# Four stacked graph layers on one core: the first tiles of the last projection between the last sums of layer 3, and the mask sums of a layer's first block between the first pair's tiles

## The chip, the cores and the metric

The kernel runs on one core of a Trainium2 chip. The core has five engines that run their own queues in order and meet through semaphores: TensorE (PE, matmul; its weight loads are shown as PEld), VectorE (DVE), ScalarE (ACT), GpSimd (POOL) and SyncE (SP, which here only issues transfers). The metric is the device time of one execution in microseconds (us), the median of several runs. Less is better.

## The reference

The input is a matrix x of 2708 rows and 512 columns and a symmetric 0/1 adjacency of 2708 x 2708 with a full diagonal. Four layers follow each other, each as x = layernorm(x + f(x, adj)). Layers 0 and 1 are sums over neighbours with linear maps. The change concerns layers 2 and 3, which are graph attention.

```python
# layer 2, and the first half of layer 3: 8 heads of 64 columns each
Wh = einsum('nf,hfo->hno', x, W)
e = leaky_relu(src[:, :, None] + dst[:, None, :], 0.2)   # src, dst: Wh times a vector, per head
attn = softmax(where(adj > 0, e, -9e15), axis=-1)
h = einsum('hnm,hmo->hno', attn, Wh)
...
# layer 3 goes on
x1 = elu(h), heads side by side                           # [2708, 512]
h2 = the same attention with one head of 512 columns, weights Wo, ao
out = relu(elu(h2) @ lin1 + b1) @ lin2 + b2
x = layernorm(x + out)
```

## The kernel before, in words

Rows are cut into NT = 22 tiles of P = 128 rows (the last has 20). The transposed mask lies in SBUF as fp8 (maskT). All phases are written one after another in one Python function. A scheduler of the framework then orders each engine's queue, so an instruction may stand earlier in its queue than its place in the text. Two things hold it: data and buffers, and chains by hand. The function pe() chains matmuls in program order, each after the one before it. A second means, tc.issue_after, places what is issued in it after a named instruction.

The order of phases for layers 2 and 3 is: project("p2"), heads_attention("a2"), project("p3"), heads_attention("a3"), project("p4"), last_attention. The last one holds the one-head attention and the two linear maps.

**project** takes the 22 input tiles one at a time. For each it has a transposed input xT, multiplies it with the weights (L561, 16 matmuls), and makes from the result the columns dcol, ucol, ecol, vcol and the values R2 that the attention uses. The helper early() makes inputs ahead of need. For p4 the input is made by elu_turned, two tiles at a time.

**heads_attention** works on two blocks of output columns: tiles 0 to 10 (1408 columns) and 11 to 21 (1300 columns). Within a block it goes by pairs of heads, four pairs a block, so eight runs. A run loops over the 22 row tiles j. For each j and each of the two heads:

- DVE makes the unnormalised weights e (L624), from a broadcast row v_bc, a column of ucol, and the mask. There are five e buffers.
- ACT makes c from e (L632, a sigmoid with a huge scale, so 0 or 1): which of the two branches of the leaky_relu holds.
- PE adds R2 times e into po (L782), 12 matmuls for the two heads.
- After every four j, PE adds c times parts_c into pd (L697, "divisors").

The softmax's divisor of each column is put together from these divisor sums and from a sum over the mask alone. The mask sums are the products of masks() (L680, 88 matmuls for a block), a copy, a small matmul (fold) and a copy into rcs (keep, L689). For the second block they stand already between the tiles of a pair, at j = 12, 16 and 20. For the first block they stand ahead of the first pair:

```python
            products, fold, keep = masks(0, pd[1])
            for step in (*products, fold, keep):
                step()
            todo = {}
```

After a pair, finish() lays its steps over the tiles of the next pair (the dictionary todo, by j): the last divisors (rest), fold, divide (which ends with a reciprocal into rcs). In layer 3 the summed features are sent to the DRAM tensor oT_dram as they stand, transposed and undivided. At the last pair of a block, spread transposes the reciprocals, copies them to a tile r and sends them, head by head, to rc_dram (L752).

**elu_turned** reads both back. It loads o from oT_dram (L833) and the reciprocals rc from rc_dram, broadcast over partitions (L835, two loads), multiplies (L837, DVE), takes exp (L838, ACT), and finishes the elu with two DVE steps (L839, L840). Its o buffers, four of two tiles each, are the last 4096 of the 10240 columns of the tile lin, which lies in memory that the attention of layer 3 has used. The first part of lin takes the weights of the first linear map, 2 MB, loaded by the GpSimd queue (L858).

The last line of project checks that all values lie in a range and counts them into okc. The sum of the counts must equal expected.

Of the kernel before, what the change touches and what calls it, by code (L numbers as in the profile page):

```python
# [2 lines left out]

# [15 lines left out]
P = 128  # L19
D = 512  # L20
# [10 lines left out]
def kernel(  # L31
# [59 lines left out]


    o_dram = dram.tile([N, D], F32, name="o_dram")
    oT_dram = dram.tile([D, N], F32, name="oT_dram")
    rc_dram = dram.tile([H, NT * P], F32, name="rc_dram")

    behind = []

# [54 lines left out]
    def early(first, n, make):  # L153

        made = {}

        def get(i, **how):
            for j in range(len(made), min(i + first + 1, n)):
                made[j] = make(j, **how)
            return made[i]  # L160
        return get
# [337 lines left out]
    rcs = late.tile([P, 2, H, 12], F32, name="rcs")  # L499
    okc = const.tile([P, 4], F32, name="okc")  # L500
    nc.vector.tensor_scalar(rdeg, iso, 0.0, None, op0=OP.is_equal, op1=OP.add, accum_out=okc[:, 3:4])
    expected = float(P * NT * (3 * H + 1))

    def split(pool, dst, src):

# [7 lines left out]
    def project(name, source, layer, v_dram, cuts, turned=None):  # L513
# [12 lines left out]
        with ExitStack() as ph:  # L526
# [5 lines left out]
            xs = early(1, NT, lambda t: source(sm, t, rows(t)))  # L532
            xTs = early(0, NT, lambda t: transposed(ahead, ps_tr, xs(t), rows(t), "xT"))
            if turned:
                twos = early(2, -(-NT // 2), lambda i: turned(sm, 2 * i, min(2 * i + 2, NT)))
                xTs = lambda t: twos(t // 2)[:, :, t % 2 * P:t % 2 * P + P]
            vrows, bs = {}, {}

            def keep_v(t):
# [52 lines left out]
                                                    -1.0, None, op0=OP.mult)  # L592
                            split(sm, pairs_c[:, a:z, :, k, 6 * k + 3:6 * k + 6], ecol[:, a:z, k::2])
            keep_v(NT - 1)
            sq = sm.tile([P, NT, H], F32, name="sq", bufs=1)
            if heads < H:
                nc.vector.memset(sq, 0.0)
            dd = dcol[:, :, :heads]
            nc.vector.tensor_mul(sq[:, :, :heads], dd, dd)
            sq = sq.rearrange("p t h -> p (t h)")  # L600
            nc.vector.tensor_scalar(sq, sq, RANGE * RANGE, None, op0=OP.is_le, op1=OP.add,
                                    accum_out=okc[:, layer:layer + 1])

# [31 lines left out]
    nb = 2  # L635
    cuts = [-((-NT * i) // nb) for i in range(nb + 1)]
    blocks = list(zip(cuts[:-1], cuts[1:]))

    def heads_attention(name, att, as_rows):

        with ExitStack() as ph:
# [56 lines left out]
            def finish(b, h0, p, pair, oT):  # L700

                t0, t1 = att.blocks[b]
                nt = t1 - t0
                feats, cols = slice(h0 * HO, (h0 + 2) * HO), slice(t0 * P, t0 * P + att.width(b))
                got = {}

                def rest():
                    divisors(b, p, pair)
                    got["dT"] = copied(p)

                def fold():
                    got["sums"] = folded(got["dT"], pick_c.rearrange("p g k q -> p (g k q)")).rearrange(
                        "p t g (k q) -> p t g k q", k=2)

                def divide():
                    sums, r = got["sums"], rcs[:, b, h0:h0 + 2, :]
                    rc = sm.tile([P, 2, 12], F32, name="rc")
                    by = rc.rearrange("p k (g t) -> p t g k", g=4)
                    nc.vector.tensor_mul(by, sums[:, :, :, :, 1],
                                         vcol[:, t0:t0 + 12, h0:h0 + 2].rearrange("p (g t) k -> p t g k", g=4))  # L720
                    nc.vector.tensor_add(by, by, sums[:, :, :, :, 0])
                    nc.vector.tensor_add(rc, rc, r)
                    nc.vector.tensor_scalar(rc, rc, 1e-30, None, op0=OP.max)
                    nc.vector.reciprocal(r, rc)

                def turn(a0):
                    ps = got[a0] = ps_t.tile([P, 512], F32, name="ps_t").rearrange("p (t c) -> p t c", c=P)
                    for t in range(a0, min(a0 + 4, nt)):
                        n = rows(t0 + t)
                        pe(nc.tensor.transpose(ps[:n, t - a0, :], oT[:, a0 // 4, (t - a0) * P:(t - a0) * P + n], ident))  # L730

                def store(a0):
                    a1, full, ps = min(a0 + 4, nt), min(t1, FULL) - t0, got[a0]
                    o = ahead.tile([P, KD, P], F32, name="xT")
                    for n, a, z in [(P, a0, min(a1, full)), (rows(NT - 1), max(a0, full), a1)]:
                        if a >= z:
                            continue
                        nc.scalar.copy(o[:n, a - a0:z - a0], ps[:n, a - a0:z - a0])
                        r0 = (t0 + a) * P
                        rows_ = o_dram[r0:r0 + (z - a - 1) * P + n, feats]  # L740
                        if n == P:
                            nc.sync.dma_start(rows_.rearrange("(t p) c -> p t c", p=P), o[:, a - a0:z - a0])
                        else:
                            nc.sync.dma_start(rows_, o[:n, a - a0])

                def spread():
                    ps = ps_t.tile([P, 512], F32, name="ps_t")
                    pe(nc.tensor.transpose(ps[:12 * H, :P], rcs[:, b].rearrange("p h t -> p (h t)"), ident))
                    r = sm.tile([12 * H, P], F32, name="r", bufs=1)
                    nc.scalar.copy(r, ps[:12 * H, :P])  # L750
                    for h in range(H):
                        nc.gpsimd.dma_start(rc_dram[h, t0 * P:t1 * P].rearrange("(t p) -> t p", p=P),  # L752
                                          r[12 * h:12 * h + nt])

                steps = {0: [rest], 4: [fold], 6: [divide]}
                if as_rows:
                    for a0 in range(0, nt, 4):
                        steps[8 + a0] = [lambda a0=a0: turn(a0)]
                        steps[9 + a0] = [lambda a0=a0: store(a0)]
                else:  # L760
                    nc.gpsimd.dma_start(oT_dram[feats, cols], oT.rearrange("p i c -> p (i c)")[:, :att.width(b)])
                    if h0 == H - 2:
                        steps[8] = [spread]
                return steps

            products, fold, keep = masks(0, pd[1])
            for step in (*products, fold, keep):
                step()
            todo = {}
            for r, (b, h0) in enumerate(runs):  # L770
                w = att.width(b)
                parts = [(c, min(c + 4 * P, w)) for c in range(0, w, 4 * P)]
# [1 line left out]
                vs = [att.load(b, h) for h in hs]  # L774
                po = [ps_o.tile([P, 512], F32, name="po", tag="po") for _ in parts]
                pair = []
                for j in range(NT):
                    es = [att.weights(b, h, j, v) for h, v in zip(hs, vs)]
                    cs = [att.above(b, h, j, e) for h, e in zip(hs, es)]
                    for i, (c0, c1) in enumerate(parts):  # L780
                        for k, (h, e) in enumerate(zip(hs, es)):
                            pe(nc.tensor.matmul(po[i][HO * k:HO * k + HO, :c1 - c0], R2[:, j, h * HO:(h + 1) * HO],  # L782
                                                e[:, c0:c1], start=(j == 0), stop=(j == NT - 1)))
                    if len(pair) == 4:
                        divisors(b, pd[r % 2], pair)
                        pair = []
                    pair.append((j, hs, cs))
                    for step in todo.get(j, ()):
                        step()
# [26 lines left out]
    def summed(sm, t, n):  # L816
# [7 lines left out]
        nc.gpsimd.dma_start(x3_dram[t * P:t * P + n, :], o)  # L824
        return o

    def elu_turned(sm, t0, t1):

        w = sum(rows(t) for t in range(t0, t1))
        cols = slice(t0 * P, t0 * P + w)  # L830
        o = lin[:, -KD * 1024:].rearrange("p (i k n) -> p i k n", i=4, k=KD)[:, t0 // 2 % 4]
        rc = sm.tile([P, KD, 2 * P], F32, name="rc2")
        nc.sync.dma_start(o[:, :, :w], oT_dram.rearrange("(k p) n -> p k n", p=P)[:, :, cols])  # L833
        for q in range(2):
            nc.sync.dma_start(rc[HO * q:HO * q + HO, :, :w],  # L835
                                rc_dram.rearrange("(k q) n -> q k n", q=2)[q, :, cols].partition_broadcast(HO))
        nc.vector.tensor_mul(o[:, :, :w], o[:, :, :w], rc[:, :, :w])  # L837
        nc.scalar.activation(rc[:, :, :w], o[:, :, :w], AF.Exp)  # L838
        nc.vector.tensor_scalar(rc[:, :, :w], rc[:, :, :w], 1.0, -1.0, op0=OP.min, op1=OP.add)  # L839
        nc.vector.scalar_tensor_tensor(o[:, :, :w], o[:, :, :w], 0.0, rc[:, :, :w], op0=OP.max, op1=OP.add)  # L840
        return o
# [116 lines left out]
    for i, source in enumerate((plain, summed)):  # L958
        with ExitStack() as ph:
            att = Weights(ph, f"a{2 + i}", blocks, vd[i])  # L960
            project(f"p{2 + i}", source, i, vd[i], blocks)
            heads_attention(f"a{2 + i}", att, i == 0)
    ph4 = fast.enter_context(ExitStack())
    att = Weights(ph4, "a4", quads, vd[2])
    lin = ph4.enter_context(tc.tile_pool(name="lin", bufs=1)).tile([P, KD * FF + KF * D + KD * 512], F32, name="lin")
# [329 lines left out]
```

## Time and profile before

| | before |
|---|---|
| median of 3 runs | 3096.92 us (3095.4 to 3097.85) |
| profiled run, span | 3089.8 us |
| PE busy | 2969.2 us, 96% |
| DVE busy | 1963.5 us, 64% |
| ACT busy | 1411.1 us, 46% |
| layers 0 and 1 and p2, first instruction to first po | 0 to about 1024 us |
| attention of layer 2, from the first po | 1024.57 to about 1587 us |
| attention of layer 3, from the first po to the last divisors | 1701.49 to 2252.62 us |
| p4, first product | 2279.76 us |

How to read it: a busy share is an average over stages with different limits. In the two attentions of eight heads PE and DVE are both almost full, and which of them sets the pace has to be read from the waits. A line such as "L561" is line 561 of the kernel; "x16" is a number of instructions; a bracket at a line's end tells how long the engine stood before it and what ended the wait. Instruction durations of one engine may overlap a little, so the spacing of two is often less than a duration.

### The profile page before, as it was taken

To read this page: it belongs to the slowest core of one execution; us is meant where nothing else is said; L and a number is where in the kernel's file an instruction comes from. 1 tells how busy PE (TensorE), PEld (TensorE's weight loads), DVE (VectorE), ACT (ScalarE), POOL (GpSimd) and SP (SyncE) were. 2 spreads that over 40 slices of the span, in tenths; PEclk is the share of its full clock that TensorE was granted. 3 is DMA by queue.
4 is the path that set the end of the run, shared out by engine and by line. 5 is a ranking of instruction groups with operands and counts; after the bars stand their busy time and mean duration, and the time that the engine had idled before them with its cause. 6 is when DMAs were issued, how large, how long until landed. Compare 5 with 4: busy or idle time off the path is not lost. (4 is left out here: it accounts for less than half of the span.)

```text
span 3089.8 us, 36801 instructions
## 1 busy us (share of the span) xinstructions
PE 2969.2 (96%) x14714; PEld 1644.4 (53%) x14714; DVE 1963.5 (64%) x2495; ACT 1411.1 (46%) x1590; POOL 239.6 (8%) x378
## 2 busy tenths in 40 slices
PE   8999999999999999999998999999969999999997
PEld 4556666448888433444466333443446455555555
DVE  5662765212233899999976999999944535344242
ACT  2431000112225699999965899999942000001001
POOL 2220010101110000000012000000000000100001
PEclk9999999999999999999999999999989999999999
DMA  6651521312222001011034000000052000000000
GB/s 142 142 124 35 121 67 38 109 60 90 73 74 84 15 29 47 28 38 34 22 107 153 29 29 28 28 27 27 18 156 63 4 14 17 31 14 15 14 21 20
DMA packets 112920, 168.93 MB, mean 55 GB/s; under 512 B 39716, under 2 KB 63141, under 8 KB 112738
## 3 DMA queue, kind: packets, MB, share of 16 engines
q1 hardware_dynamic: 84066, 105.02, 11.4%
q0 software_dynamic: 18784, 57.79, 6.5%
q10 hardware_dynamic: 9888, 3.67, 0.5%
q8 instruction: 118, 1.93, 0.2%
q14 instruction: 64, 0.52, 0.1%
HBM read 136.46 MB, written 44.64 MB: 59 GB/s over the span
## 5 line engine op out<-in xcount | busy, mean ns | idle before, releaser
L624 DVE SCALAR_TENSOR_TENSOR e<-v_bc,ucol,maskT 128x1300 f32<-128x1300 f32 (+3 forms) x836 | 1183.2, 1474 | 335.0 <-PE pn L926 318.8
L632 ACT ACTIVATE c<-e,bcol 128x1300 fp8e4<-128x1300 f32 (+1 forms) x704 | 994.6, 1424 | 82.7 <-DVE e L624 32.8
L782 PE MATMUL po<-e,R 128*64 128x512 f32 (+2 forms) x4224 | 924.9, 549 | 29.9 <-DVE e L624 28.2
L782 PEld LDWEIGHTS po<-e,R 128*64 128x64 f32 x4224 | 349.0, 136 | 573.2 <-issue 383.2
L926 PE MATMUL pn<-e,R 128*128 128x512 f32 (+1 forms) x1056 | 415.1, 544 | 0.0
L926 PEld LDWEIGHTS pn<-e,R 128*128 128x128 f32 x1056 | 192.1, 191 | 199.8 <-issue 196.7
L416 PE MATMUL acc<-yH,kT 128*128 128x512 f32 x484 | 214.8, 444 | 0.0
L894 ACT ACTIVATE w<-pl,b 128x256 f32<-128x256 f32 (+1 forms) x88 | 40.9, 465 | 373.3 <-PE pl L892 373.3
L458 PE MATMUL acc<-yL,mf 128*128 128x512 f32 x484 | 192.9, 399 | 0.0
L416 PE MATMUL acc<-yL,kT 128*128 128x512 f32 x484 | 192.3, 397 | 0.0
L458 PE MATMUL acc<-yH,mf 128*128 128x512 f32 x484 | 190.5, 394 | 0.0
L117 POOL TENSOR_TENSOR ln_rs<-ln_rs,half 128x1 f32<-128x1 f32 x88 | 54.5, 620 | 1676.4 <-DVE ln_rs L116 1674.5
L561 PE MATMUL pm<-w,xT 128*128 128x264 f32 (+1 forms) x704 | 168.3, 394 | 10.7 <-DVE R L575 5.2
L229 PE MATMUL pm<-w,xT 128*128 128x512 f32 (+1 forms) x384 | 173.2, 593 | 2.4 <-ACT xT L130 1.4
L229 PE MATMUL pm<-weight,xT 128*128 128x512 f32 (+1 forms) x352 | 162.0, 604 | 3.6 <-DVE weight L141 2.8
L321 DVE SCALAR_TENSOR_TENSOR kT<-pm,maskT 128x512 fp32r<-128x512 f32 (+1 forms) x132 | 84.8, 642 | 123.5 <-PE pm L319 123.0
L892 PE MATMUL pl<-lin 128*128 128x256 f32 (+1 forms) x704 | 154.8, 374 | 2.8 <-DVE lin L811 2.8
L901 PE MATMUL pl<-lin,w 128*128 128x512 f32 (+1 forms) x352 | 157.4, 593 | 0.0
L561 PEld LDWEIGHTS pm<-w,xT 128*128 128x128 f32 (+1 forms) x704 | 129.6, 189 | 38.0 <-issue 5.8
L892 PEld LDWEIGHTS pl<-lin 128*128 128x128 f32 x704 | 130.6, 192 | 33.4 <-issue 15.8
L455 ACT CAST mf<-maskT 128x1024 fp32r<-128x1024 fp8e4 (+1 forms) x66 | 64.4, 977 | 163.4 <-PE acc L458 154.1
L223 ACT CAST yH<-pm 128x512 fp32r<-128x512 f32 (+1 forms) x44 | 25.7, 585 | 243.6 <-PE pm L229 243.6
(186 smaller groups left out, 2619.9 us busy)
## 6 DMA issues: line engine op xcount, KB each, us to landing
rows<-x_dram SPq DMA_DIRECT2D x63, 256.0 KB
m<-in_adj_dram POOLq DMA_DIRECT2D x21, 677.0 KB, 6.2
v_bc<-v_dram SPq DMA_DIRECT2D x16, 704.0 KB
x_dram<-u POOLq DMA_DIRECT2D x42, 256.0 KB, 2.3
v_bc<-v_dram SPq DMA_DIRECT2D x16, 650.0 KB
rows<-in_x_dram SPq DMA_DIRECT2D x21, 256.0 KB
r_dram<-u POOLq DMA_DIRECT2D x21, 256.0 KB, 3.2
rows<-r_dram SPq DMA_DIRECT2D x21, 256.0 KB
```

Of the source, the lines that this page charges most:

```text
L229: order(nc.tensor.matmul(pm[:n], xT[:, k, :n], w[:, k, :], start=(k == 0), stop=(k == KD - 1)))
L321: nc.vector.scalar_tensor_tensor(kT[:, :w], cum[:, :w], KEEP, maskT[:, j, cols], op0=OP.is_le, op1=OP.mult)
L416: nc.tensor.matmul(pa[t], kT[:, (t - b[0]) * P:(t - b[0] + 1) * P], y[:, j, :], start=(j == 0 and y is yH), stop=(j == NT - 1 and y is yL))
L455: nc.scalar.copy(mf[:, :g1 - g0, :], maskT[:, g0:g1, t * P:(t + 1) * P])
L458: nc.tensor.matmul(pa, mf[:, j - g0, :], y[:, j, :], start=(j == 0 and y is yH), stop=(j == NT - 1 and y is yL))
L561: nc.tensor.matmul(pm[a][:n, :D // 2 + heads], xT[:, k, :n], w[:, k, a, :D // 2 + heads], start=(k == 0), stop=(k == KD - 1))
L624: nc.vector.scalar_tensor_tensor(e[:, :w], v[:, :w], ucol[:, j, h:h + 1], maskT[:, j, c0:c0 + w], op0=OP.max, op1=OP.mult)
L632: nc.scalar.activation(c[:, :w], e[:, :w], AF.Sigmoid, bias=bcol[:, j, h:h + 1], scale=STEP, saturate=False)
L782: pe(nc.tensor.matmul(po[i][HO * k:HO * k + HO, :c1 - c0], R2[:, j, h * HO:(h + 1) * HO], e[:, c0:c1], start=(j == 0), stop=(j == NT - 1)))
L892: nc.tensor.matmul(pl[:, :w], self.lin1[:, k, f * P:(f + 1) * P], h[:, k, :w], start=(k == 0), stop=(k == KD - 1))
L901: nc.tensor.matmul(pl[:n], gT[:, f, (t - t0) * P:(t - t0) * P + n], self.lin2[:, f, :], start=(f == 0), stop=(f == KF - 1))
L926: nc.tensor.matmul(pn[k][:, :w], R2[:, j, k * P:(k + 1) * P], e[:, :w], start=(j == 0), stop=(j == NT - 1))
```

## The change

It has two parts.

First, the mask sums of block 0 no longer stand ahead of the first pair. They are put into todo, as those of block 1 were: three groups of products after the first pair's tiles 12, 16 and 20, fold and keep in the next pair. The first pair's own sums can so begin without them, in layer 2 and in layer 3.

Second, the border between layer 3's eight-head attention and the last projection. Both DRAM tensors are split by block, so that a load of block 0 has nothing to do with block 1's stores. The input of the projection is cut into one tile, one tile, and then pairs. The two single tiles are made, with the whole of elu_turned, after tiles 10 and 14 of the last pair of layer 3, in buffers of the pool ahead ("rows" and "xT") that outlives the attention. The pairs are made as before, in lin. All loads of elu_turned are kept in the order of the text by issue_after. The tile r of spread moves to the pool ahead too. The tile sq of the range check is cut to the heads in use, with no memset, and expected follows (a one-head layer counts 1 per row tile in place of 8).

```diff
-    oT_dram = dram.tile([D, N], F32, name="oT_dram")
-    rc_dram = dram.tile([H, NT * P], F32, name="rc_dram")
+    oT_dram, rc_dram = [], []
...
+    for i, (a, z) in enumerate(blocks):
+        oT_dram.append(dram.tile([D, (z - a) * P], F32, name=f"oT_dram{i}"))
+        rc_dram.append(dram.tile([H, (z - a) * P], F32, name=f"rc_dram{i}"))
...
-                twos = early(2, -(-NT // 2), lambda i: turned(sm, 2 * i, min(2 * i + 2, NT)))
-                xTs = lambda t: twos(t // 2)[:, :, t % 2 * P:t % 2 * P + P]
+                cuts_ = [(0, 1), (1, 2)] + [(t, min(t + 2, NT)) for t in range(2, NT, 2)]
+                parts = early(2, len(cuts_), lambda i: ready[i] if i in ready else turned(sm, *cuts_[i]))
...
-            sq = sm.tile([P, NT, H], F32, name="sq", bufs=1)
-            if heads < H:
-                nc.vector.memset(sq, 0.0)
+            sq = sm.tile([P, NT * H], F32, name="sq", bufs=1)[:, :NT * heads]
...
             products, fold, keep = masks(0, pd[1])
-            for step in (*products, fold, keep):
-                step()
-            todo = {}
+            todo = {12: products[:1], 16: products[1:2], 20: products[2:], NT: [fold], NT + 2: [keep]}
...
+                if r + 1 == len(runs):
+                    for j, steps in meanwhile.items():
+                        todo[j] = todo.get(j, []) + steps
...
-                    r = sm.tile([12 * H, P], F32, name="r", bufs=1)
+                    r = ahead.tile([P, D], F32, name="rows", bufs=3)[:12 * H, :P]
...
+        n = 1 if t0 < 2 else t1 - t0
+        if n == 1:
+            o = ahead.tile([P, D], F32, name="rows", bufs=3).rearrange("p (k n) -> p k n", k=KD)
+            rc = ahead.tile([P, KD, P], F32, name="xT")
+        else:
+            o = lin[:, -KD * 1024:].rearrange("p (i k n) -> p i k n", i=4, k=KD)[:, t0 // 2 % 4]
+            rc = sm.tile([P, KD, 2 * P], F32, name="rc2")
+        for b, (a, z) in enumerate(blocks):
+            c0, c1 = max(a, t0), min(z, t1)
+            if c0 < c1:
...
+                with tc.issue_after(loads[-1].ins) if loads else nullcontext():
+                    loads.append(nc.sync.dma_start(
+                        o[:, :, to], oT_dram[b].rearrange("(k p) n -> p k n", p=P)[:, :, cols]))
+                for q in range(2):
+                    with tc.issue_after(loads[-1].ins):
+                        loads.append(nc.sync.dma_start(
+                            rc[HO * q:HO * q + HO, :, to],
+                            rc_dram[b].rearrange("(k q) n -> q k n", q=2)[q, :, cols].partition_broadcast(HO)))
...
-            heads_attention(f"a{2 + i}", att, i == 0)
+            heads_attention(f"a{2 + i}", att, i == 0, {
+                10 + 4 * t: [lambda t=t: ready.update({t: elu_turned(None, t, t + 1)})] for t in range(2)} if i else {})
```

## What was predicted

> **What bounds the kernel now.** I read the busy table first, then PE's waits, then the timeline at the two places the change touches, then the busy times by stage.
>
> ```profile
> PE 2969.2 (96%) x14714; PEld 1644.4 (53%) x14714; DVE 1963.5 (64%) x2495; ACT 1411.1 (46%) x1590; POOL 239.6 (8%) x378
> ...
> PE pm L561 <- DVE lin L840: 24.0, 1, 24.0
> ```
>
> PE carries the span, yet one wait of 24.0 us stands out: the first product of the last projection (L561) waits for the first finished tile of its input (L840). The timeline there (start, length, engine):
>
> ```profile
> 2251.80 0.82 PE L697 MATMUL pd<-c,parts_c 128*12 128x384 fp8e4 x16
> 2256.30 3.51 POOL L752 DMA_DIRECT2D rc_dram<-r  x7 [1.99 <-ACT r L750]
> 2266.81 0.51 POOL L752 DMA_DIRECT2D rc_dram<-r  x1 [7.00 <-DMA rc_dram<-r]
> 2268.77 20.89 SPq L835 DMA_DIRECT2D rc<-rc_dram  x9
> 2273.93 1.22 DVE L837 TENSOR_TENSOR lin<-lin,rc 128x1024 f32<-128x1024 f32 x1 [4.74 <-DMA rc<-rc_dram]
> 2275.22 1.28 ACT L838 ACT_TABLE_LOAD   x1 [19.20 <-DVE lin L837]
> 2279.76 9.88 PE L561 MATMUL pm<-w,lin 128*128 128x257 f32 x32 [24.05 <-DVE lin L840]
> ```
>
> The reader is to see a serial chain: divisors of the last pair, reciprocals written to DRAM, read back, four vector and scalar steps, PE. Although the first tiles belong to block 0, whose reciprocals were written 200 us earlier, they wait for block 1's write.
>
> At each layer's first pair, the DVE queue shows the second hole (layer 2, then layer 3):
>
> ```profile
> 1020.68 0.35 DVE L511 CAST parts_c<-rest 128x44 bf16<-128x44 f32 x1
> 1024.74 0.32 DVE L689 COPY rcs<-ps_t 128x96 f32<-128x96 f32 x1 [3.71 <-PE ps_t L669]
> 1027.18 6.47 DVE L624 SCALAR_TENSOR_TENSOR e<-v_bc,ucol,maskT 128x1408 f32<-128x1408 f32 x4 [2.12 <-PE po L782]
> ...
> 1699.38 0.35 DVE L511 CAST parts_c<-rest 128x44 bf16<-128x44 f32 x1
> 1701.66 0.32 DVE L689 COPY rcs<-ps_t 128x96 f32<-128x96 f32 x1 [1.93 <-PE ps_t L669]
> 1704.10 4.88 DVE L624 SCALAR_TENSOR_TENSOR e<-v_bc,ucol,maskT 128x1408 f32<-128x1408 f32 x3 [2.12 <-PE po L782]
> ```
>
> Five weight tiles e fill their buffers before this; DVE then stands until PE, busy with the mask sums, consumes the first. That matters because DVE, not PE, paces these pairs (busy us of PE, PEld, DVE, ACT, POOL in each stretch; the last lines are the border):
>
> ```profile
> 1096.00:1167.00 71.00, 69.09 (x457) 27.77 (x456) 70.24 (x50) 65.94 (x51) 0.00 (x0) 1.00 0.09 32
> 1238.00:1309.00 71.00, 69.43 (x535) 29.20 (x533) 69.27 (x49) 65.30 (x50) 0.00 (x0) 1.00 0.09 30
> 2186.00:2252.00 66.00, 63.85 (x453) 26.79 (x457) 62.65 (x47) 60.72 (x49) 0.53 (x1) 1.00 0.03 11
> ...
> 2256.00:2258.00 2.00, 0.00 (x0) 0.00 (x0) 0.00 (x0) 0.02 (x1) 1.70 (x4) 0.99 1.03 358
> 2258.00:2260.00 2.00, 0.00 (x0) 0.00 (x0) 0.00 (x0) 0.00 (x0) 1.81 (x4) 0.50 1.09 403
> ```
>
> Stretch 1238 to 1309 has 78 more matmul records, the mask sums of block 1, and DVE is as full as elsewhere: mask sums between the tiles of a running pair cost nothing there.
>
> **What the Trainium skill says.** "TensorE: Matmul & The Clock Gate", section "What's actually happening": PE falls to half clock after an idle window of about 3.4 us. The trace agrees: idle from 2255.7, clock 0.99 up to 2258, then 0.50. "ScalarE: Activation LUTs", section "What ACT_TABLE_LOAD costs": 1283 ns, and 1380 ns of drain. The trace shows the 1.28 us and no drain: the load at 1674.63 is followed by the next c at 1675.92. I take 1.28. "DMA: Bandwidth & Descriptors", section "Issuing engines are not separate DMA queues": all issuers share 16 engines. The border agrees: with DMA share 1.03 to 1.09 the small rc_dram writes wait 7.00 us.
>
> **Part 1, mask sums of block 0 (both layers).** Nothing is removed but order: 88 matmuls (5.43 us in layer 2, 3.75 in layer 3), a copy, the fold and L689 go from ahead of the first pair to its tiles 12 to 24. PE can then start po when the projection ends (1014.5, at the latest 1017) instead of at 1024.57. One step j frees two e in 2.58 us, so by about 1020 DVE can go on, and it needs them only when its splits end at 1021.03. Removed: 3.71 + 2.12 = 5.8 us of DVE idle in layer 2, 1.93 + 2.12 = 4.05 in layer 3; sum 9.9. L689's 0.32 us is only moved. The moved PE work must find room: a step needs 2.58 for po and 1.47 / 4 for the divisors, 2.95, against two e at a spacing of 1.60 (27 in 43.08 us), 3.2. Slack 0.25 x 22 = 5.5 us a pair, for 3.75 us in three pieces of at most 1.4 us, less than one e; four spare e buffers carry PE over each. Gain 9.9; low end 5 (PE starts only after block 0's parts are split, or is short of slack), high end 14 (DVE also fills its 2 us holes in the projection).
>
> **Part 2, tiles 0 and 1 in the last pair.** Added on the pacing engine: per tile a product, a min/add and a max/add of 128x512. The rows for such shapes (L870 0.684, L808 0.420, L811 0.684) give 1.79 us, 3.6 for both. ACT gets an exp (0.57, L809) with two table loads, as c uses another table: 0.57 + 2 x 1.28 = 3.1 us twice. ACT lags 1.4 us behind DVE after each; its c come at 1.37 us when it catches up (two of 1408 columns in 2.84), so it gains some 0.2 us per e and is level within 7 e, before the second tile's. DVE's min waits for that exp and the e behind it in its queue wait too; PE lives on the five buffers meanwhile. The loads (SP queue, block 0's rows, all written by 2020) land in a time when the DMA share is 0.03. I take 3.6 + 0.4 = 4 us; low 3, high 10 if every exp stalls DVE by some 3 us more.
>
> **Part 3, the border.** Let T be the end of the last divisors (2252.62 before). Before, tiles 0 and 1 are through PE at T + 37.0 (2279.76 + 9.88). After, PE takes them at once: their banks are those of po, copied out by 2252.33. Two tiles at 3.58 us end by T + 7 to T + 10.5, the later if fold and spread (to 2255.72) come first. Next is the part of tiles 2 and 3. The split DRAM tensors, and r in another pool, let its loads go at T. Their DMA work: 512 KB of o, 1.3 us at the 390 GB/s of the stretch 2258 to 2266, and two rc loads of 1.25 us (four took about 5.2 us from 2270), 3.8 in sum. They share the engines with oT's last write and the 2 MB of lin1 (11.3 us to landing), at half rate some 7.5 us; with 2 us to start and land, T + 10. Then product, exp, min and max (1.22 + 1.06 + 0.69 + 1.23, with hand-overs 4.6): T + 14.6. PE has stood over 4 us and starts cold: before, 32 matmuls took 9.88 instead of 7.0, and 16 after a 4.7 us wait at 1585 took 5.49 instead of 3.73; I take 2.3. So the equal of T + 37.0 is T + 17: gain 20. The pair of rc2 buffers then turns in about 5 + 4.6 us for two parts, 4.8 a part against PE's 7.2, and the rest runs as before. Bounds: 28 if the loads land by T + 6 and PE stays warm; 11 if tiles 2 and 3 are ready only at T + 23.
>
> The chain added by issue_after keeps SP's loads in order; what queues behind a blocked rc load is only the next part's, not yet needed. The smaller sq and its dropped memset (0.20 us) count nothing: the memset lies in the hole. The new columns of the check cost nothing.
>
> **Sum.** 3096.9 - 9.9 + 4 - 20 = 3071.0 us.
>
> **Rivals.**
> A, the border gives little: loads of tiles 2 and 3 wait for lin1 or for memory of the finished attention, so PE waits at tile 2 in place of tile 0. For it: DMA share at 1.0 until 2267. Against: only 3.8 us of transfers are needed. Gain 11: 3096.9 - 9.9 + 4 - 11 = 3080.
> B, everything overlaps better: masks 13, loads early, tiles 2 and 3 by T + 8, no cold PE (gain 27), DVE pays 3: 3060. For it: some e buffers under lin come free before T. Against: the lin1 load.
> C, slower: the two early tiles block DVE. If their loads stand in SP's queue behind one that waits for a buffer until the pair's end (SP's v_bc loads wait up to 70.3 us for an e), DVE stands about 20 us for each tile: 3096.9 - 9.9 + 40 - 20 = 3107. For it: DVE runs in order and paces the stage. Against: the pair's own v_bc loads come before its first e, so nothing need stand ahead of the new loads.
>
> **How the numbers follow.** Forecast 0.60, A 0.20, B 0.13, C 0.07. The predicted time is the forecast's, 3071. The bounds of the forecast alone (masks 5 to 14, DVE 3 to 10, border 11 to 28) are not all met at once; 3058 takes in B, 3086 takes in A with a weak mask part, and C stays outside. Faster by over 0.2% (under 3090.7) are forecast, A and B nearly whole: 0.92; same 0.03; slower 0.05.
>
> **What would show it.** Right: the 24.0 us wait of L561 gone, and one of about 4 us at tile 2 on DVE or the rc load; mask matmuls (L680) among po's; first DVE e after the splits within 1 us; two more exp and some four more table loads in the last pair, which is 4 us longer. Wrong: a new DVE wait for ACT's exp or for the loads in the last pair, PE waits at several tiles of the last projection, or first pairs longer by their mask sums.

## The result, and the profile after

| | before | after |
|---|---|---|
| median, us | 3097.39 (3095.4 to 3098.23) | 3070.84 (3068.76 to 3076.51) |
| span of the profiled run | 3089.8 | 3066.7 |

The ratio is 0.9918, 95% interval 0.9901 to 0.9935: 26.6 us less by the medians, 23.1 us between the two traces. A second measurement of the same changed kernel, told of below, gave 3072.57 us. So the gain is some 24 to 27 us.

The busy line of the page, and the waits of PE (who waited for whom: us in total, times, longest), of the kernel after. Its lines are numbered a little higher: L562 is the product that was L561, L860 the last vector step of its input.

```profile
PE 2962.6 (97%) x14714; PEld 1639.0 (53%) x14714; DVE 1959.7 (64%) x2497; ACT 1413.7 (46%) x1595; POOL 239.8 (8%) x378
...
PE pm L562 <- DVE lin L860: 11.8, 1, 11.8
```

The wait of 24.0 us is now one of 11.8. The timeline of DVE at the head of layer 2, after:

```profile
1019.38 0.26 DVE L592 TENSOR_SCALAR parts_c<-parts_m 128x132 bf16<-128x132 bf16 x1
1019.52 1.67 DVE L622 SCALAR_TENSOR_TENSOR e<-v_bc,ucol,maskT 128x1408 f32<-128x1408 f32 x1
1021.10 0.35 DVE L508 CAST parts_c<-rest 128x44 bf16<-128x44 f32 x1
1021.21 1.69 DVE L622 SCALAR_TENSOR_TENSOR e<-v_bc,ucol,maskT 128x1408 f32<-128x1408 f32 x1
...
1031.46 0.35 DVE L510 CAST parts_c<-rest 128x44 bf16<-128x44 f32 x1
...
1692.30 1.67 DVE L622 SCALAR_TENSOR_TENSOR e<-v_bc,ucol,maskT 128x1408 f32<-128x1408 f32 x1
```

The two holes of 3.71 and 2.12 us are gone. The first five e fill their buffers well ahead of this in both kernels (in layer 2 by about 990). The sixth now begins among the splits (the casts and differences that make parts_c), at 1019.52 in place of 1027.18. In layer 3 (last line) it begins 4.6 us after the last product of the projection, in place of 11.3. The mask sums (L682) stand between the divisors and the next po, here in layer 3:

```profile
1729.33 1.15 PE L699 MATMUL pd<-c,parts_c 128*12 128x384 fp8e4 x26
...
1730.48 1.62 PE L682 MATMUL pd<-maskT,parts_m 128*24 128x256 fp8e4 x30
1732.03 10.19 PE L786 MATMUL po<-e,R 128*64 128x512 f32 x48
```

And the border, after (all engines, weight loads left out):

```profile
2242.62 1.13 PE L562 MATMUL pm<-w,rows 128*128 128x257 f32 x4
2242.69 0.53 POOL L763 DMA_DIRECT2D oT_dram<-oT  x1 [65.56 <-ACT oT L796]
2242.77 0.37 SPq L849 DMA_DIRECT2D lin<-oT_dram  x1
2243.62 0.76 POOL L878 DMA_DIRECT2D lin<-in_L_gnn_lin_w_dram  x1 [0.40 <-issue]
2248.14 1.26 SPq L853 DMA_DIRECT2D rc<-rc_dram  x2
2258.28 1.23 DVE L857 TENSOR_TENSOR lin<-lin,rc 128x1024 f32<-128x1024 f32 x1 [7.39 <-DMA rc<-rc_dram]
2262.73 8.89 PE L562 MATMUL pm<-w,lin 128*128 128x257 f32 x32 [11.82 <-DVE lin L860]
...
2292.58 3.73 PE L562 MATMUL pm<-w,lin 128*128 128x257 f32 x16 [1.65 <-ACT R L580]
```

T, the end of the last divisors, is 2242.69. PE takes tile 0 at once and is through two tiles at about 2250.7. Then it stands, and tile 2 begins at T + 20.0. The rc loads of tiles 2 and 3 are issued only at 2248.14 and used at 2258.28. A later tile (2292.58) waits again.

Where the 23.1 us of the traces come from, by marks that both have (the first copy of po at each pair's end, T, and the first matmul after the projection, pk):

| stretch | change, us |
|---|---|
| start to the end of layer 2's last pair | -5.04 (the projection of layer 2 ended 0.79 later, so -5.83 for the attention) |
| to the end of layer 3's block 0 | -5.43 |
| layer 3's block 1, with the two early tiles | +0.53 |
| border and last projection, T to pk | -11.94 (T + 110.97 to T + 99.03) |
| from pk to the end | -1.23 |

### The profile page after: what moved, and what is told of

It is laid out like the page before. It is cut to its first block, busy times and chain, and to the rows that moved or that the text cites. A ratio compares the mean times of both kernels' runs of the same rounds, so it can differ in the third digit from the quotient of the medians.

```text
span 3066.7 us, 36820 instructions
## 1 busy us (share of the span) xinstructions
PE 2962.6 (97%) x14714; PEld 1639.0 (53%) x14714; DVE 1959.7 (64%) x2497; ACT 1413.7 (46%) x1595; POOL 239.8 (8%) x378
## 5 line engine op out<-in xcount | busy, mean ns | idle before, releaser
L562 PE MATMUL pm<-w,xT 128*128 128x264 f32 (+1 forms) x704 | 168.1, 393 | 10.5 <-DVE R L576 5.1
L562 PEld LDWEIGHTS pm<-w,xT 128*128 128x128 f32 (+1 forms) x704 | 129.2, 189 | 38.1 <-issue 6.3
```

Of the source, the lines that this page charges most:

```text
L562: nc.tensor.matmul(pm[a][:n, :D // 2 + heads], xT[:, k, :n], w[:, k, a, :D // 2 + heads], start=(k == 0), stop=(k == KD - 1))
```

## The experiments

Medians of the kernel before were 3094.9 to 3096.7 us beside these runs. One kernel's runs spread over some 2 to 8 us, so differences of a few us are read inside the trace. "Block 1" is the length of layer 3's block 1, between the first copies of po at its ends; "late tile" is the start of the first product fed by the loads at the border, from T; pk also from T.

| run | median | block 1 | late tile | pk |
|---|---|---|---|---|
| before | 3097.39 | 266.1 | 27.1 (tile 0) | 111.0 |
| after | 3070.84 | 266.6 | 20.0 (tile 2) | 99.0 |
| e1 masks only | 3083.9 | 266.2 | 27.0 (tile 0) | 113.0 |
| e2 border only | 3083.86 | 266.6 | 21.6 (tile 2) | 99.6 |
| e3 no early tiles | 3076.28 | 266.2 | 21.3 (tile 0) | 106.1 |
| e4 lin1 late | 3075.12 | 266.4 | 16.1 (tile 2) | 100.1 |
| e5 rc2 apart | 3067.4 | 266.4 | 17.8 (tile 2) | 93.5 |
| e6 both | 3061.76 | 266.3 | 13.3 (tile 2) | 90.1 |
| e7 four early | 3066.17 | 269.1 | 21.1 (tile 4) | 91.1 |
| e8 all | 3061.94 | 269.0 | no wait there | 85.5 |
| e9 in the pair | 3072.99 | 269.3 | 22.9 (tile 2) | 101.2 |
| e10 two pairs | 3061.1 | 269.5 | no wait there | 84.2 |
| e11 after again | 3072.57 | 266.4 | 22.5 (tile 2) | 101.6 |
| e12 both again | 3061.03 | 266.3 | 13.1 (tile 2) | 89.9 |

Traces of one border differ too. With the border of the changed kernel (after, e2, e9, e11) tile 2 starts at T + 20.0 to 22.9 and pk lies at T + 99.0 to 101.6, and the trace "after" is the earliest of the four in both. With the old border (before, e1) pk lies at T + 111.0 to 113.0. So a difference of some 2.5 us between two traces shows nothing by itself.

**The two parts apart.** e1 is the kernel before with the new todo; e2 is the changed kernel with the old lines in its place.

```diff
-            for step in (*products, fold, keep):
-                step()
-            todo = {}
+            todo = {12: products[:1], 16: products[1:2], 20: products[2:], NT: [fold], NT + 2: [keep]}
```

> The kernel before with the mask part alone: the first block's mask sums after tiles 12, 16 and 20 of the first pair, border untouched. Theory M (the parts are separate, and the mask part fills DVE's holes ahead of the first pair): the end of layer 2's pairs comes 5.8 us earlier against layer 2's entry, layer 3's about 5.4 us against its own, the border still holds the wait of 24 us; 3097 - 11 = 3086 us. Rival P (PE has no room for the sums in a running pair, and the shift seen in the changed kernel comes from elsewhere): first pairs longer by 3.7 to 5.4 us, gain under 3 us, 3094 or more.

> The changed kernel with the mask sums back ahead of the first pair, in both layers. Theory M: the 24 us wait shrinks to about 12 us at tile 2, the last block of layer 3 is longer by at most 1 us; 3097 - 13 = 3084 us. Rival P (the border gives nearly all): 3075 us or less.

e1 is 11.9 us faster than before in its comparison (ratio 0.9957, interval 0.9941 to 0.9974), e2 also 11.9 (0.9962, 0.9948 to 0.9976). Their sum, 23.8, agrees with the whole. Theory M holds and both forms of P fall: PE had room for the sums, and neither part carries the gain alone. Counted from the last product of the projection ahead of it, layer 2's attention ends 6.3 us earlier in the twelve traces with the moved sums than in the two without (5.5 to 7.9 from trace to trace), and layer 3's second pair 5.5 us earlier (5.5 to 5.6).

How PE absorbs the sums shows in the lengths of the pairs. From the projection's last product, in the traces before and after, the first pair ends only 4.6 us (layer 2) and 3.9 us (layer 3) earlier after the change. The second pair then takes 70.0 to 70.1 us in all twelve traces, and 71.5 to 71.7 in the two others: PE was some 1.6 us behind after the pair with the sums, and caught up in the next. DVE kept its pace: in layer 3 its second pair, from one wait for v_bc to the next, is 71.5 us long before and 71.8 after.

**What the split of the tensors gives, and what the early tiles.** e3 makes the input again in pairs from tile 0:

```diff
-                cuts_ = [(0, 1), (1, 2)] + [(t, min(t + 2, NT)) for t in range(2, NT, 2)]
+                cuts_ = [(t, min(t + 2, NT)) for t in range(0, NT, 2)]
...
-                10 + 4 * t: [lambda t=t: ready.update({t: elu_turned(None, t, t + 1)})] for t in range(2)} if i else {})
+                10 + 4 * t: [lambda t=t: ready.update({t: elu_turned(None, t, t + 1)})] for t in range(0)} if i else {})
```

> The changed kernel without the two early tiles: inputs of the last projection again in pairs from tile 0, all made after the attention; DRAM tensors split, r in the other pool, mask sums moved. T is the end of the last divisors. Theory M (early tiles give PE 7 us of work, while the next pair is limited by its own loads): first product of the projection at about T + 20, in place of T + 27 before; some 7 us slower than the changed kernel, 3078 us. Rival S (separating the loads from block 1's store is all that counts): the same as the changed kernel, 3071 us. Rival E (the early tiles are all, the split gives nothing): first product at T + 27, 3084 us.

The first product came at T + 21.3, as theory M had it; its wait, in e3's timeline of PE:

```profile
2264.24 10.18 PE L562 MATMUL pm<-w,lin 128*128 128x257 f32 x32 [18.16 <-DMA lin<-oT_dram]
```

(The load that the bracket names had landed by 2259.41, when DVE used it; the last DVE step of this input ended at 2264.03.) The marks of pk put 4.9 us down to the split tensors and the moved r together (T + 111.0 to T + 106.1), and 7.1 us to the two early tiles (to T + 99.0), which is two tiles of PE work. With the other traces of the same borders these are 4.9 to 6.8 and 4.6 to 7.1 us. S and E each leave one of the two out.

**Why tile 2 came at T + 20 and not at T + 14.6.** Two causes lay open in the trace: the 2 MB load of lin1 (issued at 2243.62) on the same DMA engines, and the wait of the first rc load, which the queue's waits put down to oT's store:

```profile
SPq L853 <- DMA oT_dram<-oT: 4.7, 1, 4.7
```

e4 holds lin1 back with a copy that its load must follow:

```diff
+            if self.pool:
+                nc.gpsimd.tensor_copy(self.lin1[:, 0, 0:1], dcol[:, 9, 0:1])
             nc.gpsimd.dma_start(self.lin1, l3_lin1_w.rearrange("(k p) f -> p k f", p=P))
```

> The changed kernel with the 2 MB load of lin1 held back until tile 9 of the last projection is through (a one-column copy into lin1 from dcol goes ahead of it). T is the end of the last divisors. Theory L (the loads of tiles 2 and 3 are late because they share the DMA engines with lin1): they land by T + 9 to T + 10, tile 2 starts at T + 14, in place of T + 20; 3 to 6 us faster than the changed kernel, 3066 us. Rival B (they are late because the first rc load waits for the memory of oT until oT's store has read it): that issue stays at T + 5.4, landing T + 9.5 at the earliest if the engines are free, T + 15 if they are not; tile 2 not before T + 14. The two differ in the issue time of the first rc load, and in how long it takes to land.

Both theories saw a half. The issue stayed at T + 5.7 (B), and from issue to use the loads now took 5.9 us in place of 10.1 (L), or of up to 13.0 in the other traces with this border: tile 2 at T + 16.1. But pk, at T + 100.1, did not move. In e4's timeline, where lin1 is loaded:

```profile
2292.44 1.25 SPq L853 DMA_DIRECT2D rc<-rc_dram  x2
2292.75 0.78 POOL L880 DMA_DIRECT2D lin<-in_L_gnn_lin_w_dram  x1 [0.35 <-POOL lin L879]
2303.88 1.22 DVE L857 TENSOR_TENSOR lin<-lin,rc 128x1024 f32<-128x1024 f32 x1 [5.02 <-DMA rc<-rc_dram]
2305.03 0.15 DVE L567 COPY dcol<-pm 128x1 f32<-128x1 f32 x1
2306.85 5.42 PE L562 MATMUL pm<-w,lin 128*128 128x257 f32 x16 [4.06 <-ACT R L580]
```

The rc loads issued beside lin1 take 11.4 us. DVE stands in its queue at the product that needs them (L857); behind it stands the copy of a finished tile (L567), ACT waits for that, and PE for ACT. The late load took back what it had given.

e5 puts rc2 into columns of lin that lin2 fills only later, instead of memory shared with oT:

```diff
-            rc = sm.tile([P, KD, 2 * P], F32, name="rc2")
+            rc = lin[:, KD * FF:KD * FF + KD * 512].rearrange("p (i k n) -> p i k n", i=2, k=KD)[:, t0 // 2 % 2]
```

> The changed kernel with the two rc2 buffers in the part of lin that the second linear map's weights take later, away from the memory of oT. T is the end of the last divisors. Theory B (the first rc load waits for the memory of oT, to T + 5.4): its issue comes to about T + 1, and with lin1 still on the engines it lands by T + 11, tile 2 starts at T + 15 to T + 16 in place of T + 20; 4 us faster than the changed kernel, 3067 us. Rival L (lin1's load alone sets it): issue earlier, landing still at T + 14 to T + 15, tile 2 at T + 19, 3070 us.

The first rc load is issued at T + 0.5, as B had it, but takes 12.8 us to its use, for now it meets both oT's store and lin1: tile 2 at T + 17.8, between the two theories. pk came 5.5 us earlier, more than tile 2 gained: the second waits of the changed kernel (2287.09 and 2292.58) are gone as well.

e6 has both edits, with tile 20 in place of tile 9 in e4's copy, so that lin1 meets no other load.

> The buffers of rc2 as in the run before, and lin1's 2 MB held back until tile 20 of the last projection is through, so that its transfer meets no other. Theory L + B (both causes hold, and e4 gave its 4 us back because lin1 met the loads of later tiles): first rc load lands by T + 6 to T + 7, tile 2 at T + 11, no wait of over 2 us in the later tiles, the last projection ends 8 to 9 us earlier against T than in the changed kernel; 3062 us. Rival D (the transfers of the projection are the bound whatever their order): tile 2 early, but later waits give it back, under 3 us in all, 3068 us or more.

```profile
2245.20 2.47 SPq L853 DMA_DIRECT2D lin<-rc_dram  x2
2253.53 1.23 DVE L857 TENSOR_TENSOR lin<-lin 128x1024 f32<-128x1024 f32 x1 [4.10 <-DMA lin<-rc_dram]
2257.97 9.42 PE L562 MATMUL pm<-w,lin 128*128 128x257 f32 x32 [2.76 <-DVE lin L860]
```

Tile 2 at T + 13.3 (T is 2244.69), 2.3 us later than expected, and pk 8.9 us earlier than in the changed kernel, as L + B had it; no later tile waits. D falls. So both causes are shown: e4 and e5 each take one away, and tile 2 comes 6.7 us earlier without both (9.4 from e11 to e12). The two rc loads still take 8.3 us from issue to use; they now meet oT's store, which lands at T + 5.4. e11 and e12 are the changed kernel and e6 once more, beside each other.

> The changed kernel itself, beside the others on one chip: 3071 us.

> The kernel of e6 (rc2 away from oT, lin1 late, two early tiles) once more, beside the changed kernel on one chip: 8 to 9 us faster than it, 3062 us.

3072.57 us (ratio to before 0.9924, 0.9910 to 0.9937) against 3061.03 (0.9888, 0.9873 to 0.9903): e6 beats both kernels, by some 11 us here and 9 in the first measurements.

**What an early tile costs.** e7 makes four tiles early: the first four of cuts_ are single, the steps begin after tile 5, the fourth uses a buffer of the other name, r has its own tile. e8 is e7 with e6's edits.

> The changed kernel with four early tiles in place of two (from tile 5 of the last pair on, the fourth in a buffer of the other name, r in a tile of its own). Theory M: PE works until T + 14.5, the pair of tiles 4 and 5 is ready at about T + 20, the wait falls from 12 to about 5.5 us, and the two more tiles cost the pacing DVE 0.5 to 1.5 us: 5 to 6 us faster than the changed kernel, 3065 us. Rival V (early tiles cost DVE their full 1.8 us each, as the prediction had it, plus stalls for exp): the last block of layer 3 is longer by 4 us or more, and the gain is under 3 us.

> Four early tiles, rc2 away from oT and lin1 after tile 20, together. Theory L + B + M: the next pair is ready at T + 11 to T + 12, before PE is through four tiles at T + 14.5: no wait, PE never cold, the projection ends at about T + 81 in place of T + 99; 16 to 18 us faster than the changed kernel, 3054 us. Rival D (transfers are the bound): waits at later tiles, the projection ends after T + 90, 3062 us or more.

e7's pk is 7.9 us earlier, but block 1 is 2.5 us longer, so 5.4 remain: the total of theory M, with a DVE cost between its own and V's. In e8 PE finds tile 4 ready; two waits of 1.1 and 1.2 us follow at later tiles, and pk is T + 85.5, not T + 81. Against e6 that is 4.7 us won and 2.7 lost in block 1, and the medians show nothing of it. The 3054 us that were expected were missed by 8. By the marks, e8's trace against the one after has 13.6 us won from T to pk and 2.4 lost in block 1; another 1.7 us are lost ahead of block 1 and 3.0 behind pk, stretches at which the edit does not aim and in which e6 and e12, one kernel, differ by 2.4 and 3.2.

In the changed kernel two tiles had cost only 0.5 us of block 1 (its kernels without early tiles, before, e1 and e3, take 266.1 to 266.2 us, those with two 266.3 to 266.6, but for e9). Where their steps stood, in its timeline of block 1:

```profile
2039.13 1.28 DVE L857 TENSOR_TENSOR rows<-rows,xT 128x512 f32<-128x512 f32 x2
2043.64 0.63 ACT L858 ACTIVATE xT<-rows 128x512 f32<-128x512 f32 x1
2106.09 0.75 DVE L859 TENSOR_SCALAR xT<-xT 128x512 f32<-128x512 f32 x2
2106.76 0.68 DVE L860 SCALAR_TENSOR_TENSOR rows<-rows,xT 128x512 f32<-128x512 f32 x1
2173.11 0.68 DVE L860 SCALAR_TENSOR_TENSOR rows<-rows,xT 128x512 f32<-128x512 f32 x1
```

The scheduler had spread the vector steps over the borders of the pairs (2039, 2106, 2173); only the second exp stands inside a pair, at 2066.43. At these borders, before, DVE waited for the next pair's v_bc. First the kernel before, from 1980 to 2247, then the one after:

```profile
DVE e L624 <- DMA v_bc<-v_dram: 3.8, 4, 1.0
```

```profile
DVE rc L721 <- PE ps_t L671: 5.6, 1, 5.6
DVE e L622 <- ACT oT L796: 0.6, 1, 0.6
```

Of the 3.8 us, 0.9 belong to the head of block 1, where the kernel after waits as well (0.85 us, at 1973.21, ahead of its window). The three borders held 2.9 us before and 0.6 after; the 5.6 us lie behind the last pair. e9 ties the steps to their place in the text:

```diff
-                        todo[j] = todo.get(j, []) + steps
+                        todo[j] = todo.get(j, []) + [lambda step=step: placed(step) for step in steps]
...
+            def placed(step):
+                with tc.issue_after(att.made.ins):
+                    step()
```

> The changed kernel with the steps of the two early tiles tied to their place in the text: they follow the weights of tiles 10 and 14 of the last pair. (In the changed kernel the scheduler had put the vector steps at the borders between the pairs of the last block.) Theory H (the early tiles were nearly free because their vector steps stood where DVE waits for a v_bc load anyway): the last pair is longer by 3.3 to 7 us, as two tiles at 1.8 us and waits for exp; 3075 us. Rival N (DVE has that much room anywhere in the pair): the last pair longer by under 1 us, 3071 us.

```profile
2209.22 0.69 DVE L861 TENSOR_TENSOR rows<-rows,xT 128x512 f32<-128x512 f32 x1
2212.79 0.43 DVE L863 TENSOR_SCALAR xT<-xT 128x512 f32<-128x512 f32 x1
2214.61 0.69 DVE L864 SCALAR_TENSOR_TENSOR rows<-rows,xT 128x512 f32<-128x512 f32 x1
```

In e9 they stand inside the pair, without a wait, and the last pair takes 69.9 us in place of 67.0: 2.9 more, under H's range but nearer to it than to N, and the waits at the three borders are back (1.06, 1.06 and 0.88 us). The medians do not show it (3072.99 against 3072.57); 3 us is within their spread. e10, with four early tiles over two pairs, was to bring e8's loss down.

> Four early tiles, rc2 away from oT, lin1 after tile 20, as in e8, with the first two tiles' steps put into the last pair but one, so that four tiles have two more borders between pairs. Theory H: the last pair loses the 2.4 us that e8 had over the changed kernel, the rest as e8; 3059 us. Rival N: as e8, 3062 us.

It did not: the last pair still takes 69.2 us, the one before it 67.6. H's second claim fell. The traces show that hardly anything moved: the first two tiles' products stand at the same border in both (2040.82 in e8, 2041.99 in e10), and of the third and fourth tile all vector steps but one product stand inside the last pair in both (2216 to 2235 in e8, 2218 to 2237 in e10). One step did move, the second tile's last, from a border (2174.78 in e8) into the last pair but one (2138.88 in e10), which is 0.6 us longer for it. Why the scheduler leaves them there stays open.

## Why the prediction was right, and where it was not

The time came within a microsecond, and that is in part luck. The border gave 8 us less than its term; the early tiles cost 3.5 us less and the mask sums gave 1.4 us more than theirs. The three add up to some 3 us that the median of the first measurement does not show.

- **Part 1, mask sums: right.** 9.9 us predicted; 5.83 and 5.43 in the traces, 6.3 and 5.5 over all runs. The mechanism is the one argued: DVE's holes close and PE absorbs the sums. The holes alone are 5.83 and 4.05 us, as predicted. What makes it more is that e now run among the splits: over the first two pairs DVE is busy 1.6 us (layer 2) and 1.4 us (layer 3) less, with the same 118 instructions. The prediction has no such term; its high end named the holes in the projection. In layer 2 the waits of DVE at the ends of the first two pairs grew from 1.7 to 3.1 us and took most of that back.
- **Part 2, the early tiles: the term of 4 us was mis-sized.** It measured 0.5. The DVE work was as priced (1.28 + 0.75 + 0.68 + 0.68 = 3.4 us, and two exp with four table loads of 1.28), but the vector steps stood at the borders of the pairs, where 2.9 us of waiting for v_bc lay in the profile before. e9 shows the price where they cannot hide: 2.9. The error was to take the place in the text for the place in the queue.
- **Part 3, the border: the term of 20 us was mis-sized.** It measured 11.9. Tile 2 came at T + 20.0 against T + 14.6, for the first rc load was not issued at T, as the step had it, but at T + 5.4, behind oT's store (e5, e6). lin1's share of the engines was in the sum and is real (e4). Another 3.1 us were lost at later tiles, where the prediction let "the rest run as before": two of them start 4.79 and 5.49 us after the one ahead, in place of 3.58. e5 and e6 have no such waits. The cold start cost 1.7 us (8.89 against 7.16 for two warm tiles), where 2.3 were expected. When the clock falls is less sure than the prediction has it: in its own trace the last matmul ends at 2255.72 and the clock is 0.50 from 2258, so after 2.3 us, not 3.4; in the kernel after PE ends at 2250.91 and the clock is still 0.99 up to 2256.
- **Rival A came true at the border**, with its mechanism (the loads of tiles 2 and 3 wait for lin1 and for memory of the finished attention, PE waits at tile 2) and its gain of 11. Its total, 3080 us, failed mainly by the other two terms. One of the prediction's signs of being wrong, waits of PE at several tiles of the last projection, is there too (2287.09 and 2292.58).
- **Rivals B and C** did not come true: the border gave 11.9 us and not B's 27, and there was no DVE wait for the early loads, which the SP queue issued by 2012.

With the measured terms the sum is 3096.9 - 11.3 + 0.5 - 11.9 = 3074.2, some 3 us above the median; the traces' tail and entry differ by another 0.4 us, and the rest is within the spread of runs.

## What to carry to other kernels

When work that PE can do at any time stands ahead of a loop that another engine paces, and PE has room inside the loop, put it between the loop's tiles: here the holes that it made for the pacing engine (5.83 and 4.05 us) were as long as its matmuls (5.43 and 3.75). At a border between stages, ask for each load of the next stage what frees its memory and what else is on the DMA engines then: a buffer that lies under the last store, and a large load that is needed much later, delayed the next stage's first loaded tile by 6.7 to 9.4 us together here. Extra work on the pacing engine is cheap only where that engine waits, so count those waits before pricing it, and expect the next two tiles to cost more than the first two (2.5 us in e7 against 0.5).

## What was not expected of the hardware

An rc load (256 KB, broadcast to partitions) moves at about half the rate of a plain one with the DMA engines busy throughout: 207 GB/s from 2256 to 2258 against 398 from 2246 to 2248 in the kernel after. Beside a 2 MB load the first pair of them takes 10.1 to 13.0 us from issue to use (after, e2, e3, e5, e7, e9, e11), 7.8 to 8.3 without that load but with oT's store (e6, e8, e10, e12), and 5.9 with neither (e4).
